# Attention layer of a four-layer network: Q, K and V in seven block products each, with t in the output's pixel order

## The chip, the cores and the metric

The kernel is one program on 1 core of one Trainium2 chip. The metric is device microseconds (us) of that core from launch to end; lower is better. Shown times are medians over several executions.

## The reference

Four layers follow one another, each of the form `x = x + layer(groupnorm(x))` on a float32 image batch of 8 x 16 x 256 x 256. Layer 0 is a convolution with capsule routing, layer 1 a convolution over spline bases, layer 2 an attention, layer 3 a circular 3x3 convolution. The change is in layer 2 alone:

```
hn, wn = (H // P, W // P)          # P = 16: 256 patches of 16 x 16 pixels
N = hn * wn;  ed = P * P
emb = _pos_embeddings(C * N, ed).reshape(C, N, ed)
patches = x.reshape(B, C, hn, P, wn, P).transpose(0, 1, 2, 4, 3, 5).reshape(B, C, N, ed)
t = (patches + emb[None]).transpose(0, 1, 3, 2)
Q = t @ Wq.T + bq
K = t @ Wk.T + bk
V = t @ Wv.T + bv
score = jnp.einsum('bcph,bcpg->bchg', K, Q) / np.float32(HID ** 0.5)
A = jax.nn.sigmoid(score)
out = jnp.einsum('bcph,bchg->bcpg', V, A)
```

For each of the 8 x 16 = 128 pairs of image and channel ("heads" below), t, Wq, Wk, Wv, score and A are 256 x 256 matrices. So a head has five products of 256 x 256 by 256 x 256, all in float32.

## The kernel before, in words

The four layers run one after the other. All matmuls are float32, and the profile shows each as two records on TensorE, each with its own weight load.

**Layer 2** is the method `layer2`. It loops over images and, within an image, over 16 channels, and calls `attend` once for each head. A 256-row operand lies in SBUF as two halves of 128 partitions. In one head:

- VectorE (DVE) makes t from the patches `pt` by one subtract-and-multiply (L1525), and GpSimd (POOL) adds the position table `emb` (L1529).
- Q and K come together: four matmuls of 512 columns into two PSUM tiles `pqk` (L1535); DVE adds the bias and writes `qk` (L1536).
- V comes transposed: four matmuls of 256 columns into `pv` (L1542); ScalarE (ACT) adds the bias in four pieces that also put V's columns in pixel order (L1546).
- Scores: four matmuls of 256 columns into `psc` (L1550), and one sigmoid on ACT (L1558).
- Output: four matmuls of 256 columns into `po` (L1562). DVE adds the residual and writes the row tile `y` (L1567), takes its statistics (L1574, L1575), POOL copies the two edge columns (L1576, L1577), and SyncE (SP) issues the store of `y` to the scratch array `x3` (L1578).

**Order.** In layer 2 only SP's queue is written out by hand (`manual_schedule(engines={SP})`); on the other engines the framework's scheduler orders the instructions. PE's order comes out as pqk x3, pv x4, psc x4, pqk x1 (of the next head), po x4, so that work of the next head stands between a head's scores and its output.

**Buffers.** The PSUM pool has two buffers of each of `pqk`, `pv`, `psc` and `po`, all eight banks. In SBUF the pools `l2_t` and `l2_mid` have two buffers each, except `y`, which has three: head i's `y` can be written when the store of head i-3 has landed.

**SP's queue.** Besides the stores it issues the residual rows (`rows`, four channels at a time, at channels 2, 6, 10 and 14), and at channel 3 the whole patches of the next image (`patches`, two DMAs, L1427), which land in the one of the two `pt` tiles that is not in use. In the last image it fetches the first inputs of layer 3 instead (`first3`, channels 4 to 12). Its order around channel 3 is: the store of channel 2, the two patch loads, the store of channel 3.

**Statistics.** The statistics of the layer's input come in two parts: those of the last image are finished during image 1 (`stats2_steps`, all steps at once), and layer 3's during the last image (`stats3`).

Of the kernel before, what the change touches and what calls it, by code (L numbers as in the profile page):

```python
# [10 lines left out]
F32 = mybir.dt.float32  # L11
AF = mybir.ActivationFunctionType
ALU = mybir.AluOpType
AX = mybir.AxisListType
PSUM = bass.MemoryType.PSUM
DRAM = bass.MemoryType.DRAM

B, C, H, W = 8, 16, 256, 256
P = 128
WP = W + 2  # L20
# [101 lines left out]
def _embedding():  # L122

    n = 256
    pos = np.arange(C * n, dtype=np.float32)[:, None]
    step = np.float32(-(np.log(10000.0) / n))
    div = np.exp(np.arange(0, n, 2, dtype=np.float32) * step).astype(np.float32)
    ang = (pos * div).astype(np.float32)
    emb = np.zeros((C * n, n), np.float32)
    emb[:, 0::2] = np.sin(ang)  # L130
    emb[:, 1::2] = np.cos(ang)
    emb = emb.reshape(C, 2, P, 2, 8, 16)
    return np.ascontiguousarray(emb.transpose(2, 1, 0, 4, 3, 5)).reshape(P, 2, C, n)


def _layout(w0, bw, sw, sc, bias, wq, bq, wk, bk, wv, bv, w3):
# [156 lines left out]
class _Net:  # L293
# [1138 lines left out]
    def layer2(self, images=range(B), channels=range(C)):  # L1432

        nc, tc = self.nc, self.tc
        images = list(images)
        with ExitStack() as st:
            self.tpool = st.enter_context(tc.tile_pool(name="l2_t", bufs=2))
            one = st.enter_context(tc.tile_pool(name="l2_one", bufs=1))
            load = st.enter_context(tc.tile_pool(name="l2_load", bufs=2))
            mid = st.enter_context(tc.tile_pool(name="l2_mid", bufs=2))  # L1440
            wqk, wv, bqk, bv = (self.w2[name] for name in ("qk", "v", "bqk", "b2v"))
            self.pt.append(one.tile([P, 2, C, 8, 32], F32, name="pt1"))
            emb = one.tile([P, 2, C, 256], F32, name="emb")
            first = load.tile([P, 4, 16, 2, 16], F32, name="res2")
            nc.sync.dma_start(out=emb[:, :, 1:4], in_=self.d["emb"][:, :, 1:4])
            nc.sync.dma_start(
                out=first.rearrange("p c n k j -> p c (n k j)"),
                in_=self.x2[images[0]][0:4].rearrange("c r h n k j -> (r h) c (n k j)"),
            )
            nc.sync.dma_start(out=emb[:, :, 4:C], in_=self.d["emb"][:, :, 4:C])  # L1450
            psum = st.enter_context(tc.tile_pool(name="l2_ps", bufs=2, space=PSUM))
            stats = self.st3

            def bank():
                t = []

                def get():
                    if not t:
                        t.append(psum.tile([P, 512], F32, name="pb2", tag="po"))
                    return t[0]  # L1460

                return get

            def patches(b):

                pt = self.pt[b % 2]
                for half in range(2):
                    self.patch(b, half, 0, C)
                return pt

            def rows(b, c):

                res = load.tile([P, 4, 16, 2, 16], F32, name="res2")
                nc.sync.dma_start(
                    out=res.rearrange("p c n k j -> p c (n k j)"),
                    in_=self.x2[b][c : c + 4].rearrange("c r h n k j -> (r h) c (n k j)"),
                )
                return res

            pts, ress = {images[0]: self.pt[images[0] % 2]}, {(images[0], 0): first}  # L1480
            with tc.manual_schedule(engines={mybir.EngineType.SP}):
                for n, b in enumerate(images):
                    after = images[n + 1] if n + 1 < len(images) else None
                    for c in channels:
                        if c in (2, 6, 10):
                            ress[b, c // 4 + 1] = rows(b, c + 2)
                        if c == 3 and after is not None:
                            pts[after] = patches(after)
                        if c == 14 and after is not None:
                            ress[after, 0] = rows(after, 0)  # L1490
                        if c == 2 and n == 1:

                            last, steps = self.stats2_steps(self.small, "g2b", bank)
                            for _, _, run, _ in steps:
                                run()
                        if c == 0 and after is None:
                            self.bc3 = self.stats3(bank, "g3a")
                        if 4 <= c < 13 and after is None:
                            self.first3(images[:2], c - 4)
                        bc = self.bc2 if after is not None else last  # L1500
                        e = self.emb0 if c == 0 else emb[:, :, c]
                        self.attend(mid, psum, b, c, pts[b], ress[b, c // 4], e, wqk, wv, bqk, bv, bc, stats)

    def first3(self, images, part):

# [5 lines left out]
    def weights3(self, ws, stat, b):  # L1511
        self.nc.vector.scalar_tensor_tensor(
            ws, self.w3, stat[0][:, 1, b : b + 1], self.k["ident3"], ALU.mult, ALU.add
        )

    def stats3(self, bank, name):
        out, steps = self.stats3_steps(self.small, name, bank)
        for _, _, run, _ in steps:
            run()
        return out  # L1520

    def attend(self, mid, psum, b, c, pt, res, emb, wqk, wv, bqk, bv, bc, stats):
        nc = self.nc
        t = self.tpool.tile([P, 2, 8, 32], F32, name="t")
        nc.vector.tensor_scalar(  # L1525
            t, pt[:, :, c], bc[:, 0, b, c : c + 1], bc[:, 1, b, c : c + 1], ALU.subtract, ALU.mult
        )
        t = t.rearrange("p h r f -> p h (r f)")
        nc.gpsimd.tensor_tensor(t, t, emb, ALU.add)  # L1529

        qk = mid.tile([P, 2, 512], F32, name="qk")
        for k in range(2):
            ps = psum.tile([P, 512], F32, name="pqk")
            for n in range(2):
                nc.tensor.matmul(ps, t[:, n, k * P : (k + 1) * P], wqk[:, n, :], start=n == 0, stop=n == 1)  # L1535
            nc.vector.tensor_tensor(qk[:, k, :], ps, bqk, ALU.add)  # L1536

        pv = psum.tile([P, 2, 256], F32, name="pv")
        vt = mid.tile([P, 2, 2, 8, 2, 8], F32, name="vt")
        for k in range(2):  # L1540
            for n in range(2):
                nc.tensor.matmul(pv[:, k], wv[:, n, k * P : (k + 1) * P], t[:, n, :], start=n == 0, stop=n == 1)  # L1542
        for k in range(2):
            src = pv[:, k].rearrange("p (r i o s) -> p o s i r", r=8, i=2, o=2)
            for o in range(2):
                nc.scalar.activation(vt[:, k, o], src[:, o], AF.Identity, bias=bv[:, k : k + 1])  # L1546
        ps = psum.tile([P, 2, 256], F32, name="psc")
        for k in range(2):
            for n in range(2):
                nc.tensor.matmul(  # L1550
                    ps[:, k],
                    qk[:, n, 256 + k * P : 256 + (k + 1) * P],
                    qk[:, n, 0:256],
                    start=n == 0,
                    stop=n == 1,
                )
        a = mid.tile([P, 2, 256], F32, name="a")
        nc.scalar.activation(a, ps, AF.Sigmoid, scale=1.0 / 16.0)  # L1558
        po = psum.tile([P, 2, 256], F32, name="po")
        for o in range(2):  # L1560
            for k in range(2):
                nc.tensor.matmul(  # L1562
                    po[:, o], vt[:, k, o].rearrange("p s i r -> p (s i r)"), a[:, k, :], start=k == 0, stop=k == 1
                )
        y = mid.tile([P, 2, WP], F32, name="y2", bufs=3)
        rows = y[:, :, 1 : 1 + W]
        nc.vector.tensor_tensor(  # L1567
            rows.rearrange("p o (n j) -> p o n j", j=16),
            po.rearrange("p o (n j) -> p o n j", j=16),
            res[:, c % 4].rearrange("p n k j -> p k n j"),  # L1570
            ALU.add,
        )
        i = b * C + c
        nc.vector.bn_stats(stats[0][:, i, :], rows)  # L1574
        nc.vector.bn_aggr(stats[1][:, :, i], stats[0][:, i])  # L1575
        nc.gpsimd.tensor_copy(y[:, :, 0:1], y[:, :, W : W + 1])  # L1576
        nc.gpsimd.tensor_copy(y[:, :, WP - 1 : WP], y[:, :, 1:2])  # L1577
        nc.sync.dma_start(out=self.x3[b][:, c].rearrange("r h k w -> r h (k w)"), in_=y.rearrange("p k w -> p (k w)"))  # L1578

    def fetch3(self, engines, b, xs, part=range(9)):

# [175 lines left out]
def _arrays(  # L1759
# [31 lines left out]
        )  # L1791
    )
    return {"x": np.ascontiguousarray(x), "consts": _consts(), "emb": _embedding(), **made}


# [14 lines left out]
```

## Time and profile before

| | us |
|---|---|
| three runs: lowest, median, highest | 6235.46, 6244.17, 6245.69 |
| the profiled execution | 6237.4 |
| its span in the profile | 6235.3 |
| layer 0, about | 121 to 3243 of the span |
| layer 1, about | 3311 to 4865 |
| layer 2, first to last `y` | 4879.5 to 5997.4 |
| layer 3, about | 6003 to 6235 |
| PE busy in 4880 to 5997 (1117 us) | 1114.59 |
| DVE, ACT, POOL busy there | 422.86, 229.18, 197.61 |

The mean granted TensorE clock is 0.987 of full speed, and 1.00 in layer 2. The span is the time from the first to the last instruction that the profiler saw; 2.1 us of the execution lie around it. A profile line gives line, engine, operation, out<-in, shapes, count, busy time and the mean of one in ns, then the idle time before it and who ended it. A busy PE is a modelled figure, since matmuls overlap; the spacing of their starts says more.

### The profile page before, as it was taken

The numbers are of one execution on the slowest core, as the hardware profiler recorded it, in microseconds if no ns is written. First come the engines' busy times: TensorE is split into PE (matmuls) and PEld (weight loads), VectorE is DVE, ScalarE is ACT, GpSimd is POOL, SyncE is SP. The second block draws the span as 40 slices with busy tenths as digits, with TensorE's granted clock in tenths as the row PEclk, the third lists the DMA queues.
The fourth block names the chain that finished last, engine by engine and source line by source line (L and its number), as shares of the span: only waits on it lengthen the run. The fifth ranks groups of instructions, "written<-read, shape, count | busy, mean of one in ns | idle before, by whom it ended". The sixth has DMA issues, their size and how long they took to land.

```text
span 6235.3 us, 111335 instructions
## 1 busy us (share of the span) xinstructions
PE 5930.8 (95%) x44488; PEld 2760.5 (44%) x44488; DVE 4895.1 (79%) x5771; ACT 3073.6 (49%) x4858; POOL 3593.7 (58%) x3040
## 2 busy tenths in 40 slices
PE   2999999999999999999968999999999999999998
PEld 0344444444444444444423444444444666666652
DVE  5799999999999999999968999999999433333321
ACT  0444544444454445444427888888888222111221
POOL 0588888888888888888873333434443111111123
PEclk9999999999999999999978999999999999999999
DMA  7455555555555555555516555555557443444358
GB/s 286 120 137 126 144 140 134 132 144 137 130 139 142 136 126 146 138 133 133 129 40 194 177 175 176 179 175 173 175 177 191 116 90 85 89 94 103 87 183 255
DMA packets 408790, 902.08 MB, mean 145 GB/s; under 512 B 62034, under 2 KB 195762, under 8 KB 364882
## 3 DMA queue, kind: packets, MB, share of 16 engines
q1 hardware_dynamic: 364434, 831.69, 48.8%
q10 hardware_dynamic: 33984, 34.08, 1.7%
q0 software_dynamic: 9856, 29.20, 1.7%
q8 instruction: 351, 5.75, 0.4%
q14 instruction: 165, 1.35, 0.1%
HBM read 684.09 MB, written 210.77 MB: 144 GB/s over the span
## 4 chain that ended last, share of the span: by engine, by line
PE 59%; DVE 26%; issue 7%; DMA 4%; POOL 3%; ACT 1%; SPq 0%; DVEq 0%; POOLq 0%; ACTq 0%
PE rb L831 8%; PE cv L587 7%; PE pqk L1535 7%; DVE bases L1089 7%; PE pl L733 6%; DVE e L1079 4%; PE cv L591 4%; PE po L1562 4%; PE cv L550 4%; PE pv L1542 4%; PE psc L1550 4%; PE p L1627 3%; DVE pr L723 2%; DVE a L1079 2%; DVE e L1058 2%
## 5 line engine op out<-in xcount | busy, mean ns | idle before, releaser
L1112 PE MATMUL ps<-bases,tw 128*32 128x512 f32 (+1 forms) x13824 | 1360.1, 546 | 16.5 <-POOL bases L1081 6.5
L851 POOL TENSOR_TENSOR dd<-dd 128x1024 f32<-128x1024 f32 x512 | 1210.9, 2365 | 70.9 <-DVE dd L842 65.6
L1081 POOL TENSOR_TENSOR bases<-e,a 128x1024 f32<-128x1024 f32 (+1 forms) x264 | 621.1, 2375 | 925.6 <-DVE e L1079 925.6
L723 DVE TENSOR_TENSOR pr<-v,fb 128x2048 f32<-128x2048 f32 (+1 forms) x512 | 1020.8, 2014 | 17.1 <-PE pl L733 12.6
L1112 PEld LDWEIGHTS ps<-bases,tw 128*32 128x32 f32 x13824 | 597.7, 109 | 800.3 <-issue 483.3
L842 DVE SCALAR_TENSOR_TENSOR dd<-rb,v 128x1024 f32<-128x1024 f32 x768 | 906.5, 1214 | 8.9 <-POOL dd L851 3.3
L851 POOL TENSOR_TENSOR s<-s,dd 128x512 f32<-128x512 f32 x512 | 647.0, 1274 | 15.1
L831 PE MATMUL rb<-rs,ct_fold 32*128 32x512 f32 x3072 | 592.9, 634 | 25.6 <-DVE pr L723 20.2
L1546 ACT ACTIVATE vt<-pv,w_b2v 128x128 f32<-128x128 f32 x512 | 146.1, 368 | 839.6 <-PE pv L1542 839.6
L733 PE MATMUL pl<-pr,ct_fold 128*32 128x512 f32 x3584 | 506.9, 603 | 4.3 <-DVE pr L723 4.3
L587 PE MATMUL cv<-kt,w 128*128 128x512 f32 x1024 | 497.2, 608 | 11.0 <-DMA kt<-d 9.8
L851 POOL TENSOR_TENSOR s<-v,dd 128x512 f32<-128x512 f32 x256 | 328.6, 1283 | 292.5 <-DVE dd L842 292.5
L1535 PE MATMUL pqk<-w_qk,t 128*128 128x512 f32 x1024 | 482.7, 594 | 4.6 <-POOL t L1529 4.6
L550 PE MATMUL cv<-kt,w 128*128 128x512 f32 x1024 | 477.4, 609 | 2.5 <-DMA kt<-d 2.5
L1567 DVE TENSOR_TENSOR y<-po,res 128x512 f32<-128x512 f32 x128 | 88.5, 691 | 490.1 <-PE po L1562 476.0
L1529 POOL TENSOR_TENSOR t<-t,emb 128x512 f32<-128x512 f32 x128 | 162.1, 1267 | 515.8 <-DVE t L1525 501.4
L1089 DVE SCALAR_TENSOR_TENSOR bases<-xr,xm,bases 128x1024 f32<-128x1024 f32 (+1 forms) x264 | 446.5, 1729 | 0.3 <-POOL bases L1081 0.3
L596 ACT COPY v<-cv 128x1024 f32<-128x1024 f32 x256 | 251.8, 1007 | 303.1 <-PE cv L591 303.1
L1066 ACT ACTIVATE sq<-a 128x1024 f32<-128x1024 f32 (+1 forms) x264 | 263.8, 999 | 230.2 <-DVE a L1058 229.5
L831 PEld LDWEIGHTS rb<-rs,ct_fold 32*128 32x128 f32 x3072 | 226.1, 185 | 325.5 <-issue 129.3
L697 PEld LDWEIGHTS fb<-f,ct_fold 64*128 64x128 f32 x3072 | 208.7, 188 | 310.5 <-issue 177.0
L842 DVE SCALAR_TENSOR_TENSOR dd<-r,v 128x512 f32<-128x512 f32 x256 | 176.9, 691 | 190.8 <-PE r L831 176.3
(281 smaller groups left out, 10164.7 us busy)
## 6 DMA issues: line engine op xcount, KB each, us to landing
xr<-x1p SPq DMA_DIRECT2D x120, 1024.0 KB
kt<-d SPq DMA_DIRECT2D x256, 387.0 KB
kt<-d SPq DMA_DIRECT2D x128, 516.0 KB
d<-dn ACTq DMA_DIRECT2D x64, 516.0 KB
kr<-d SPq DMA_DIRECT2D x128, 258.0 KB
kt<-d SPq DMA_DIRECT2D x128, 258.0 KB
x<-y SPq DMA_DIRECT2D x128, 258.0 KB
xs<-in_x_dram SPq DMA_DIRECT2D x16, 2048.0 KB
```

Source lines behind the costliest of these rows:

```text
L550: nc.tensor.matmul(ps[g]()[:, n], w[:, 0], t[:, a : a + 2, 0:W], start=False, stop=True)
L587: nc.tensor.matmul(ps()[:, n], w2[:, 0, j, :], t[:, a : a + 2, 0:W], start=True, stop=False)
L723: nc.vector.tensor_tensor(pr()[:, :n].rearrange("p n (r w) -> p n r w", w=W), v[h]()[:, 4 * g : 4 * g + n].rearrange("p n (r w) -> p n r w ...
L733: nc.tensor.matmul(pl()[at : at + 32], sel[:, g, h, :], pr()[:, t, :], start=h == 0 and g == 0, stop=h == 1 and (g == 1 or t == 3),)
L831: nc.tensor.matmul(r()[:, n], spread[at, g, h, :], rs()[at], start=True, stop=True)
L842: nc.vector.scalar_tensor_tensor(dd()[:, :n], r()[:, :n], 1.0 / B, v[h]()[:, a : a + n], ALU.subtract, ALU.mult)
L851: op("POOL", us, lambda: nc.gpsimd.tensor_tensor(out[0](), a[0](), b[0](), ALU.add), a[1] + b[1], out[1])
L1079: nc.vector.tensor_tensor(q, q, part[4 + k], ALU.mult)
L1081: nc.gpsimd.tensor_tensor(ring[n % 3][:, 0, p : p + m, 1 : 1 + W], rows(e), rows(a), ALU.subtract)
L1089: nc.vector.scalar_tensor_tensor(r, rows(part[1]), xm[:, b : b + 1], v, ALU.is_gt, ALU.mult)
L1112: nc.tensor.matmul(out if k is None else out[:, k], lhs, rhs, start=start, stop=stop, skip_group_check=True)
L1535: nc.tensor.matmul(ps, t[:, n, k * P : (k + 1) * P], wqk[:, n, :], start=n == 0, stop=n == 1)
```

## The change

Q and K are treated as the product of t (256 x 256) with the two weight matrices, each cut into 2 x 2 blocks, and so is V. Instead of the eight block products of the schoolbook method, seven are made, of sums of blocks; the blocks of the result are sums of these. The four sums of t's blocks, `ds`, are made once for each head on POOL and serve Q, K and V. The sums of the weights' blocks, `wt` and `wu`, are made once for the layer on DVE. Q's and K's weights are the two column blocks (of 256 columns) of one 256 x 512 matrix; a block product has 256 columns there, and 128 for V. Some block products land in a PSUM tile that is read by DVE first and is accumulated into after that (`rest`, `values_rest`).

The columns of t and of `emb` now lie in the pixel order of the output, so DVE makes t in two instructions that read `pt` in strides, and V needs no reordering.

`attend` is gone. The order of all engines is written out by hand: in the step of head i, t and `ds` of head i+1, the products of head i, the output of head i-1, the scores of head i. `psum` has one buffer of each tile (`po`: two), `qk`, `a`, `u2` and `g2` have one, and `y` has two instead of three. The statistics' steps are spread, one PE step for each head.

```diff
-    return np.ascontiguousarray(emb.transpose(2, 1, 0, 4, 3, 5)).reshape(P, 2, C, n)
+    return np.ascontiguousarray(emb.transpose(2, 1, 0, 5, 3, 4)).reshape(P, 2, C, n)
...
-            psum = st.enter_context(tc.tile_pool(name="l2_ps", bufs=2, space=PSUM))
+            psum = st.enter_context(tc.tile_pool(name="l2_ps", bufs=1, space=PSUM))
...
+            wt = one.tile([P, 4, 256], F32, name="wt")
+            nc.vector.tensor_tensor(wt[:, 0], k0, q0, ALU.subtract)
+            nc.vector.tensor_tensor(wt[:, 1], k1, wt[:, 0], ALU.subtract)
...
+            def prepare(b, c):
...
+                t = ts[b, c] = self.tpool.tile([P, 2, 256], F32, name="t")
+                for h in range(2):
+                    nc.vector.tensor_scalar(
+                        t[:, h].rearrange("p (n i r) -> p n i r", i=2, r=8),
+                        pts[b][:, h, c].rearrange("p r (i n) -> p n i r", i=2),
...
+                nc.gpsimd.tensor_tensor(t, t, self.emb0 if c == 0 else emb[:, :, c], ALU.add)
+                d = sums[b, c] = self.tpool.tile([P, 4, P], F32, name="ds")
+                a11, a12, a21, a22 = t[:, 0, :P], t[:, 1, :P], t[:, 0, P:], t[:, 1, P:]
+                nc.gpsimd.tensor_tensor(d[:, 0], a21, a22, ALU.add)
+                nc.gpsimd.tensor_tensor(d[:, 1], d[:, 0], a11, ALU.subtract)
+                nc.gpsimd.tensor_tensor(d[:, 2], a11, a21, ALU.subtract)
+                nc.gpsimd.tensor_tensor(d[:, 3], a12, d[:, 1], ALU.subtract)
...
+            def product(b, c):
...
+                mm(ps[0], t[:, 0, :P], q0, True, True)
+                mm(ps[1], d[:, 1], wt[:, 1], True, True)
+                mm(ps[2], d[:, 2], wt[:, 2], True, True)
+                mm(ps[3], d[:, 0], wt[:, 0], True, True)
...
+                nc.vector.tensor_tensor(u, ps[0].unsqueeze(1).to_broadcast([P, 2, 256]), both, ALU.add)
+                nc.vector.tensor_tensor(u, ps[1].unsqueeze(1).to_broadcast([P, 2, 256]), u, ALU.add)
+                nc.vector.tensor_tensor(last, ps[2], u[:, 1], ALU.add)
+                nc.vector.tensor_tensor(last, ps[3], last, ALU.add)
...
+            def rest(b, c):
...
+                mm(ps[0], t[:, 1, :P], q1, False, True)
+                mm(ps[2], t[:, 1, P:], wt[:, 3], False, True)
+                mm(ps[3], d[:, 3], k1, False, True)
+                nc.vector.tensor_tensor(qk[:, 0, :256], ps[0], bqk[:, :256], ALU.add)
+                nc.vector.tensor_tensor(qk[:, 1, :256], ps[2], u[:, 0], ALU.add)
+                nc.vector.tensor_tensor(qk[:, 0, 256:], ps[3], u[:, 1], ALU.add)
+
+            def values(b, c):
...
+                mm(pv[:, 0], v00, t[:, 0, :P], True, True)
+                mm(pv[:, 1], wu[:, 1], d[:, 1], False, True)
+                mm(pv[:, 2], wu[:, 2], d[:, 2], False, True)
+                mm(pv[:, 3], wu[:, 0], d[:, 0], False, True)
...
+                nc.scalar.activation(g, pv[:, 0], AF.Identity)
+                nc.vector.tensor_tensor(g, pv[:, 1], g, ALU.add)
+                nc.vector.tensor_tensor(last, pv[:, 2], g, ALU.add)
+                nc.vector.scalar_tensor_tensor(last, pv[:, 3], bv[:, 1:2], last, ALU.add, ALU.add)
...
+            def values_rest(b, c):
...
+                mm(pv[:, 0], v10, t[:, 1, :P], False, True)
+                mm(pv[:, 2], wu[:, 3], t[:, 1, P:], False, True)
+                mm(pv[:, 3], v11, d[:, 3], False, True)
+                nc.scalar.activation(vt[:, 0, :P], pv[:, 0], AF.Identity, bias=bv[:, 0:1])
+                nc.vector.scalar_tensor_tensor(vt[:, 0, P:], pv[:, 2], bv[:, 0:1], g, ALU.add, ALU.add)
+                nc.vector.scalar_tensor_tensor(vt[:, 1, :P], pv[:, 3], bv[:, 1:2], g, ALU.add, ALU.add)
...
-        y = mid.tile([P, 2, WP], F32, name="y2", bufs=3)
+                y = mid.tile([P, 2, WP], F32, name="y2", bufs=2)
...
-            with tc.manual_schedule(engines={mybir.EngineType.SP}):
+            with tc.manual_schedule():
+                prepare(*todo[0])
+                for i, (b, c) in enumerate(todo):
...
+                    if i + 1 < len(todo):
+                        prepare(*todo[i + 1])
+                    product(b, c)
+                    values(b, c)
+                    rest(b, c)
+                    values_rest(b, c)
+                    if i:
+                        output(*todo[i - 1])
+                    step(late)
+                    step(after3)
+                    score(b, c)
+                output(*todo[-1])
```

`score` and `output` hold the same matmuls, sigmoid, residual add, statistics, edge copies and store as `attend` did.

## The prediction

> **What bounds the kernel now.** I read the table of windows first, by layer:
>
> ```profile
> 4880.00:5997.00 1117.00, 1114.59 (x4123) 763.27 (x4121) 422.86 (x791) 229.18 (x645) 197.61 (x379) 1.00 0.41 94
> ```
>
> In layer 2 (columns: window, us, then PE, weight loads, DVE, ACT, POOL, clock, DMA share, GB/s) PE is busy all the time at full clock and DVE for 38% of it. Then the timeline of one head, PE and DVE rows:
>
> ```profile
> 5208.31 0.55 DVE L1525 TENSOR_SCALAR t<-pt,g2a_bc 128x512 f32<-128x512 f32 x1 [1.11 <-PE pv L1542]
> 5209.76 1.02 PE L1535 MATMUL pqk<-w_qk,t 128*128 128x512 f32 x2
> 5210.67 2.00 PE L1562 MATMUL po<-a,vt 128*128 128x256 f32 x8
> 5212.50 2.74 PE L1535 MATMUL pqk<-w_qk,t 128*128 128x512 f32 x6
> 5212.70 0.69 DVE L1567 TENSOR_TENSOR y<-po,res 128x512 f32<-128x512 f32 x1 [3.85 <-PE po L1562]
> 5213.43 0.69 DVE L1574 BATCH_NORM_STATS2 st<-y 128x6 f32<-128x512 f32 x1
> 5215.08 1.89 PE L1542 MATMUL pv<-t,w_v 128*128 128x256 f32 x8
> 5216.80 0.59 PE L1550 MATMUL psc<-qk 128*128 128x256 f32 x2
> 5217.08 0.55 DVE L1525 TENSOR_SCALAR t<-pt,g2a_bc 128x512 f32<-128x512 f32 x1 [1.11 <-PE pv L1542]
> ```
>
> The period is 5217.08 - 5208.31 = 8.77 us. PE starts follow without holes: six records of 512 columns from 5212.50 to 5215.08, 0.429 us each; eight of 256 from 5215.08 to 5216.80, 0.216 each. A head has 8 and 24: 3.43 + 5.18 = 8.61, and about 0.16 is lost where `po` waits for the sigmoid. DVE idles 3.85 us before `y`. So PE's stream is the bound, and DVE has slack.
>
> SP's queue around channel 3 of image 3, and DVE's `y` there:
>
> ```profile
> 5319.02 0.57 SPq L1578 DMA_DIRECT2D x<-y  x1
> 5320.14 15.78 SPq L1427 DMA_DIRECT2D pt<-x  x2
> 5336.03 15.28 SPq L1578 DMA_DIRECT2D x<-y  x3
> 5344.24 0.69 DVE L1567 TENSOR_TENSOR y<-po,res 128x512 f32<-128x512 f32 x1 [3.85 <-PE po L1562]
> 5353.59 0.69 DVE L1567 TENSOR_TENSOR y<-po,res 128x512 f32<-128x512 f32 x1 [4.42 <-DMA x<-y]
> ```
>
> The patches' two issues hold SP for 15.8 us, so channel 3's store, whose `y` was made at 5326.70, is issued at 5336.03; it lands at 5353.5 by its semaphore. Three heads later the `y` that takes its buffer starts at 5353.59, released by that DMA: with three buffers this just fits.
>
> **The change part by part.**
>
> *PE's work.* Q and K: 7 x 2 records of 256 columns instead of 8 of 512: 3.02 for 3.43 us. V: 7 x 2 records of 128 columns instead of 8 of 256. Nearest row, 96 columns with full 128x128 weights:
>
> ```profile
> L1210 PEld LDWEIGHTS ps<-bases,ct_ident x18: 190/192/192, 3305.0 to 3306.9; 128*128 128x128 f32 x18
> L1210 PE MATMUL ps<-bases,ct_ident x18: 246/275/276, 3305.1 to 3306.9; 128*128 128x96 f32 x18
> ```
>
> The starts stand 0.112 apart (L1202, 144 columns: 0.122), although a load takes 0.19: loads overlap each other and the matmuls. So V is 14 x 0.112 = 1.57 for 1.73. With scores and output (3.45) PE has 8.05 for 8.61 us: 0.56 less. The Trainium skill, "TensorE: Matmul & The Clock Gate", "What overlaps and what doesn't", says that a weight load overlaps a matmul in flight only if their row groups differ. All of V's loads take all rows; by that rule each record costs a load of some 0.11 more, 14 x 0.11 = 1.5 us a head, +197 us in all. The row shows full-array loads hidden, and I take the row.
>
> *DVE's work.* Rows: from PSUM 512 elements 0.69 (L1536, L1567), 256 0.425 (L1338), 128 0.277 (L1355), with a scalar 0.282 (L665). In the trace an independent DVE instruction starts 0.08 before the one ahead ends, one that needs its result 0.034 after, and 0.104 after where it also waits for another engine through a wait of its own (L787 behind L786). Per head: t twice, u 2 x 0.69, six of 256, five of 128, y, statistics 0.87: some 7.2 us for 3.5. Still below PE's, but now in a chain.
>
> *The chain.* PE's order is products, V's first four, the rest, V's rest, output of i-1, scores. V's rest must wait until DVE has read all of `pv`. From the head's start: products 4 x 0.432 and V 4 x 0.224 end at 2.62, `pv` complete at 2.78; ACT copies g (0.04 + 0.36) to 3.18; DVE adds pv1, pv2, pv3 (0.03 + 0.277 + 0.034 + 0.277 + 0.034 + 0.282) to 4.11; PE sees it and loads weights (0.10 + 0.11) at 4.33, where the stream would have been at 3.92: 0.4 us idle. Then 0.67 + 1.73 + 1.73: period 8.46.
> The second loop is DVE's: `y` of i-1 starts 0.27 after output's end, at 7.0; y and statistics 1.55, t twice, u 0.80 + 0.80, last 0.53 + 0.35, and only then pv1. With t at 0.41 (256 elements, L1094) pv1 may start at 3.2 of the next head, just when g is there. t's price is not in the trace, since it now reads with strides: 0.28 (L1058, 256 elements) to 0.546 (today's 512, no gain). At 0.28 the period stays 8.46, at 0.546 it is 8.74. By the nearest row 8.47. Strides and the waits behind PE's semaphores can only add: I take 8.55, with ends 8.42 and 8.80. 127 periods x (8.55 - 8.77) = -28 us (-44 to +4).
>
> *POOL.* Four `ds` of 0.456 (L675) more a head, 3.5 us of 8.55, done by 4.3 of the head before: hidden by a whole head. Without that cover products 2 to 4 would wait about 1 us a head.
>
> *`y` with two buffers.* Head i's `y` now waits for the store of i-2. SP's order around the patches is unchanged, one store between. In the trace the store of channel 3 lands later than the second next `y` starts, in images 0 to 6, by 2.1, 10.1, 1.6, 9.3, 1.5, 9.4, 1.7: 35.6 us (e.g. 5353.5 - 5344.24). A shorter period makes that `y` due three periods after the patches' start, 0.22 x 3 earlier: +4.6. All DVE work is behind that `y`, and PE's rest of the next head waits for DVE: no slack in the loop beyond 0.1, so +40 us. Less than zero it can't be; the upper end is 50.
> *The clock.* In the three long ones PE stands for about 8 us. After an idle time of 4.59:
>
> ```profile
> 4866.56 5.12 PE L1535 MATMUL pqk<-w_qk,t 128*128 128x512 f32 x8 [4.59 <-POOL t L1529]
> ```
>
> Eight records go from 4866.56 to 4871.52, 4.96 for 3.43: 1.5 us at half clock. 3 x 1.5 = +4.5 (0 to 6).
>
> *Ends.* Start: the first products wait for `ds` (two POOL steps of 0.53 behind t) and `wt`, and the first output is one step later: first `y` +2. End: the last output follows its own scores, 4.5 instead of a period: -4. Statistics: spread, but ACT's two table loads of 1.28 and the sigmoid's reload stand ahead of the next g and delay V's rest by some 2.9 us, twice; before, the two places cost 1.8 and 4.2: 0 (-2 to +2). `wt` and `wu`, 8 instructions, some 2 us once, lie beside POOL's first t and `ds`. Layer 3 is untouched.
>
> *Sum* against the profiled execution (6237.4): -28 + 40 + 4.5 + 2 - 4 = +14.5, so 6252. The median of the runs is 6.8 above it; there the same difference gives 6259.
>
> **The rivals.**
> *Main (0.52):* period 8.45 to 8.65, stalls as worked out: +4 to +25. What can be told from no change here is 0.2%, 12.5 us.
> *A, faster (0.22):* the late stores cost less than the heads gain. If channel 3's store lands before its buffer is wanted in most images, only the period counts: 127 x -0.22 - 2 = -30, 6214. It decides below 28 us of stalls. For it: in even images only 1.5 to 2.1 us are missing. Against: the patches' issue of 15.8 us and the order on SP are the same, and a shorter period makes it worse.
> *B, DVE becomes the bound (0.22):* t at no gain and a few waits more: period 8.80 to 9.0, +41 at the low end and +62 at the high: 6285 to 6306. For it: eleven dependent links, and a sum of 7.2 of 8.5. Against: each link has a row.
> *C, V's weight loads are exposed (0.04):* period about 10, some +200, 6440. L1210 speaks against it.
> That the change does not do what it says is no rival: the number of matmuls is in the code.
>
> **How the numbers follow.** The main case gives 6259. The range leaves out half of A's better part and C: 6222 to 6308. Of the main case two fifths lie within 12.5 us, of A a quarter. Slower 0.58, same 0.26, faster 0.16.
>
> **What would show it.** Right: starts of `y` 8.45 to 8.65 apart in most heads; idle PE of about 0.4 us before V's rest, released by DVE; in each of images 0 to 6 one `y` released by the DMA of a store, 2 us late in even images and 9 to 10 in odd ones, with PE idle and slow records behind the long ones; `pv` records 0.112 apart. Wrong: no `y` released by a DMA, or one that PE doesn't feel (A); DVE without idle time before `y` and `u` waiting for DVE alone (B); `pv` records over 0.2 apart (C).

## The result

| | us | against the kernel before |
|---|---|---|
| before, median of 4 runs | 6244.93 (6235.46 to 6246.46) | 1 |
| after, median of 4 runs | 6277.74 (6275.0 to 6278.53) | 1.0059 (95%: 1.0044 to 1.0074) |
| predicted | 6259 (6222 to 6308) | |

The changed kernel is slower by 0.59%: 32.8 us between the medians. The profiled execution took 6278.5 us, 41.1 more than that of before, where the prediction's sum gave 14.5. Of the difference 3.3 us lie before layer 2 and -2.8 after it; the rest is layer 2 and its start: from the first to the last `y` it takes 1153.2 us instead of 1117.9.

The table of windows of the changed kernel, for layer 2 (the columns are those of the row shown of before):

```profile
4888.00:6041.00 1153.00, 1084.15 (x5627) 897.79 (x5625) 883.06 (x2175) 165.53 (x389) 416.29 (x879) 0.99 0.40 91
```

PE was busy in all but 2.4 us of 1117; now it stands for 69 of 1153, though it has less to do. DVE went from 38% to 77%. The clock is no longer 1.00 throughout. So the layer has lost its plain bound, and the next views must say what PE waits for. The waits of the changed kernel in layer 2 (in all, times, longest):

```profile
DVE y L1609 <- issue: 91.5, 117, 1.6
...
DVE y L1609 <- DMA x<-y: 34.1, 5, 11.2
...
PEld pq L1520 <- DVE u L1534: 31.6, 9, 9.5
...
PE pv L1520 <- DVE vt L1567: 29.0, 122, 0.2
```

Two different things are here. 122 times PE waits 0.24 us ahead of V's rest for DVE: in nearly every head. And five times `y` waits for the store that frees its buffer, up to 11.2 us, and PE waits for `u`, which stands behind that `y` on DVE, up to 9.3. The five are the `y` of channel 4 in images 1, 2, 3, 5 and 6. In images 0 and 4 the same `y` is late too, by 2.6 and 2.1 us, but this view names another releaser there.

The first, in the timeline of one head of the changed kernel:

```profile
5203.15 1.89 PE L1604 MATMUL po<-a,vt 128*128 128x256 f32 x8
...
5205.14 0.69 DVE L1609 TENSOR_TENSOR y<-po,res 128x512 f32<-128x512 f32 x1 [0.78 <-issue]
...
5206.60 0.59 PE L1520 MATMUL pq<-w_qk,t 128*128 128x256 f32 x2
5206.69 0.90 DVE L1503 TENSOR_SCALAR t<-pt,g2a_bc 128x256 f32<-128x256 f32 x2
...
5207.49 0.69 DVE L1534 TENSOR_TENSOR u<-pq,w_bqk 128x512 f32<-128x512 f32 x1
...
5210.18 0.67 PE L1520 MATMUL pq<-w_qk,ds 128*128 128x256 f32 x2
...
5210.59 0.35 DVE L1567 SCALAR_TENSOR_TENSOR vt<-pv,w_b2v,vt 128x128 f32<-128x128 f32 x1
...
5211.09 0.46 PE L1520 MATMUL pv<-t,w_v 128*128 128x128 f32 x2 [0.24 <-DVE vt L1567]
...
5211.83 1.89 PE L1604 MATMUL po<-a,vt 128*128 128x256 f32 x8
```

This is a closed loop through DVE and PE. `y` (5205.14) is followed on DVE, with gaps of at most 0.11 us, by its statistics, t, u, two additions of `qk` and those of `pv` as far as L1567 (5210.59, 5.45 later); V's rest on PE follows at 5211.09 (0.50); output stands behind V's rest (5211.83, 0.74); and an undelayed `y` starts 1.99 after output does, as 5205.14 - 5203.15 shows for the output ahead of it. 5.45 + 0.50 + 0.74 + 1.99 = 8.68, and the starts of `y` are 8.67 to 8.68 apart in most heads. The PE stream has a hole in it: the last two records of the rest start at 5210.18 and take 0.43, so V's rest could start at 5210.61 and starts 0.48 later.

The second, around channel 4 of image 3 in the changed kernel (SP's queue, DVE, PE):

```profile
5332.06 14.76 SPq L1427 DMA_DIRECT2D pt<-x  x1
...
5346.93 19.84 SPq L1620 DMA_DIRECT2D x<-y  x3
...
5365.10 0.69 DVE L1609 TENSOR_TENSOR y<-po,res 128x512 f32<-128x512 f32 x1 [11.24 <-DMA x<-y]
...
5368.18 1.22 PE L1520 MATMUL pq<-w_qk,t 128*128 128x256 f32 x2 [9.29 <-DVE u L1534]
...
5369.50 1.22 PE L1520 MATMUL pq<-wt,t 128*128 128x256 f32 x2
```

The issue of the second patch load lasts until 5346.82; that of the store of channel 2, behind it, begins at 5346.93, and the store has landed at 5364.98 by its semaphore; the `y` of channel 4, which takes that buffer, starts at 5365.10. DVE keeps its order, so t, u and the additions start after that, and PE stands for 9.29 us and then runs its records at half speed (1.22 for two records that take 0.60 in other heads; the granted clock is 0.50 from 5361.5 to 5371.7).

### The profile page after: what moved, and what is told of

The parts are those of the page before. It is cut to its first block, busy times and chain, and to the rows that moved or that the text cites. A ratio compares the mean times of both kernels' runs of the same rounds, so it can differ in the third digit from the quotient of the medians.

```text
span 6276.5 us, 117259 instructions
## 1 busy us (share of the span) xinstructions
PE 5906.9 (94%) x46024; PEld 2902.3 (46%) x46024; DVE 5368.3 (86%) x7187; ACT 3010.6 (48%) x4602; POOL 3821.4 (61%) x3552
## 4 chain that ended last, share of the span: by engine, by line
PE 46%; DVE 35%; issue 9%; DMA 5%; POOL 3%; ACT 2%; DVEq 0%; SPq 0%; POOLq 0%; ACTq 0%
PE rb L831 8%; PE cv L587 7%; DVE bases L1089 7%; PE pl L733 6%; DVE e L1079 4%; PE cv L591 4%; PE cv L550 4%; PE p L1717 3%; DVE pr L723 2%; PE po L1604 2%; DVE a L1079 2%; DVE a L1058 2%; DVE e L1058 2%; PE pv L1520 2%; PE fb L697 2%
## 5 line engine op out<-in xcount | busy, mean ns | idle before, releaser
L1112 PE MATMUL ps<-bases,tw 128*32 128x512 f32 (+1 forms) x13824 | 1360.4, 545 | 15.9 <-POOL bases L1081 6.5
L596 ACT COPY v<-cv 128x1024 f32<-128x1024 f32 x256 | 251.9, 1008 | 302.4 <-PE cv L591 302.4
L1618 POOL COPY y<-y 128x2 f32<-128x2 f32 x128 | 24.1, 189 | 521.0 <-DVE y L1609 521.0
L1048 ACT ACTIVATE d<-xr,bd,sd 128x1024 f32<-128x1024 f32 (+1 forms) x264 | 319.1, 1209 | 14.2 <-DMA xr<-x1p 14.2
L572 ACT COPY v<-cv 128x1024 f32<-128x1024 f32 x256 | 258.1, 1008 | 139.4 <-PE cv L550 139.3
L550 PEld LDWEIGHTS cv<-kt,w 128*128 128x128 f32 x1024 | 184.5, 190 | 290.9 <-issue 281.8
```

The source lines that it names most:

```text
L550: nc.tensor.matmul(ps[g]()[:, n], w[:, 0], t[:, a : a + 2, 0:W], start=False, stop=True)
L1112: nc.tensor.matmul(out if k is None else out[:, k], lhs, rhs, start=start, stop=stop, skip_group_check=True)
```

## The experiments

The main theory: the period is set by the loop above, which runs through DVE; the stalls come from the late stores, and cost what they do because all of DVE's work stands behind `y`. Its rivals: PE's own stream sets the period (as before); the buffers alone make the stall, whatever the order; the stores are late because of bytes, not because of SP's queue.

Layer 2 is read from the starts of `y` in each profile: the first to the last (free of what layers 0, 1 and 3 do), the median of the 127 distances, and the distances that exceed it. The ratios are against the runs of the kernel before on the same chip (medians 6238.2, 6238.8 and 6237.8 us in three groups); in them the changed kernel's 1.0059 would be 6275.

| kernel | time, us | ratio (95%) | first to last `y` | period |
|---|---|---|---|---|
| before | | 1 | 1117.9 | 8.77 |
| after | | 1.0059 (1.0044 to 1.0074) | 1153.2 | 8.68 |
| 1: three buffers of y | 6238.0 | 0.9997 (0.9989 to 1.0005) | 1113.3 | 8.63 |
| 2: before, two buffers | 6241.5 | 1.0006 (0.9998 to 1.0015) | 1122.7 | 8.77 |
| 3: t without strides | 6264.0 | 1.0038 (1.0025 to 1.0050) | 1136.6 | 8.50 |
| 4: one more product | 6281.9 | 1.0069 (1.0055 to 1.0082) | 1158.2 | 8.68 |
| 5: late y at channel 4 | 6253.8 | 1.0022 (1.0014 to 1.0030) | 1127.9 | 8.68 |
| 6: loads apart | 6237.3 | 0.9994 (0.9986 to 1.0003) | 1116.5 | 8.68 |
| 7: 1, and output ahead of V's rest | 6161.1 | 0.9872 (0.9856 to 0.9889) | 1042.5 | 8.04 |
| 8: 7, and t on ACT | 6161.7 | 0.9873 (0.9859 to 0.9888) | 1036.9 | 8.04 |
| 9: 6, and output ahead of V's rest | 6159.4 | 0.9871 (0.9855 to 0.9888) | 1038.5 | 8.05 |
| 10: 7, and loads apart | 6154.1 | 0.9864 (0.9849 to 0.9879) | 1035.1 | 8.04 |
| 11: 9, no root in the statistics | 6153.9 | 0.9863 (0.9848 to 0.9878) | 1031.7 | 8.05 |

### 1. Three buffers of y

```diff
-                u = mid.tile([P, 2, 256], F32, name="u2", bufs=1)
-                qk = qks[b, c] = mid.tile([P, 2, 512], F32, name="qk", bufs=1)
+                qk = qks[b, c] = mid.tile([P, 4, 256], F32, name="qk", bufs=1)
+                u = qk[:, 1:3]
...
-                y = mid.tile([P, 2, WP], F32, name="y2", bufs=2)
+                y = mid.tile([P, 2, WP], F32, name="y2", bufs=3)
```

> The changed kernel with three buffers for y again; to find the room, u lies in the two middle quarters of qk, and nothing else is moved. Theory 1 (with two buffers, the y of channel 5 waits for channel 3's late store, and that wait is on the path): the stalls of 35 to 43 us of images 0 to 6 go, so 6235 to 6245 us, -33 to -43 against the changed kernel and within 0.2% of the kernel before; no y is released by a DMA for more than 2 us in all, and y's period stays 8.67. Theory 2 (the stalls are only where waiting becomes visible, and the heads that follow would have stood anyway for POOL or for the loads of patches): at most -10 us, about 6268, and idle time of the same length appears before t, ds or the products.

From 1.0059 to 0.9997, and 39.8 us less in layer 2, as theory 1 has it. Of these, 127 x 0.045 = 6 are a shorter period (`y` starts 0.72 us after DVE's last work instead of 0.78) and 34 are stalls. The waits of this kernel in layer 2 have instead of 34.1 us in five:

```profile
DVE y L1609 <- DMA x<-y: 5.8, 2, 3.2
```

With three buffers images 3 and 5 still lose 1.9 and 2.4 us at channel 5, more than was expected; that a head of 8.63 leaves a little less room than one of 8.77 would explain it, and was not tested. The stalls did not come back elsewhere.

### 2. Two buffers in the kernel before

```diff
-        y = mid.tile([P, 2, WP], F32, name="y2", bufs=3)
+        y = mid.tile([P, 2, WP], F32, name="y2", bufs=2)
```

> The kernel before with two buffers of y instead of three: that one part of the change alone. Theory 1: the y of channel 5 waits for channel 3's store by the 35.6 us read from the trace of before. The kernel before has 3.85 us of idle DVE ahead of y and its output stands a step earlier against PE's stream, so a wait of about 2 us may be hidden in part: +30 to +45 us, 6275 to 6290. Theory 2 (TensorE's stream goes on while y waits, because po has two buffers): under +10 us, 6255 at most.

Theory 1 fails here: no change that can be told from zero, and 4.8 us in layer 2. The wait itself is there. The `y` of channel 5 comes 3.1 us late in images 0, 2, 4 and 6 and 9.8 to 10.6 late in images 1, 3 and 5; but the next one or two distances are short by almost all of it (18.70, 1.87, 7.09 in image 3, which is 27.66 where three heads take 26.31). DVE's rows there, and PE's scores:

```profile
5347.00 0.55 DVE L1525 TENSOR_SCALAR t<-pt,g2a_bc 128x512 f32<-128x512 f32 x1 [1.11 <-PE pv L1542]
5352.25 0.69 DVE L1536 TENSOR_TENSOR qk<-pqk,w_bqk 128x512 f32<-128x512 f32 x1 [4.71 <-PE pqk L1535]
5353.97 0.69 DVE L1536 TENSOR_TENSOR qk<-pqk,w_bqk 128x512 f32<-128x512 f32 x1 [1.02 <-PE pqk L1535]
5361.38 0.69 DVE L1567 TENSOR_TENSOR y<-po,res 128x512 f32<-128x512 f32 x1 [6.72 <-DMA x<-y]
...
5363.25 0.66 DVE L1567 TENSOR_TENSOR y<-po,res 128x512 f32<-128x512 f32 x1
...
5365.28 2.22 PE L1550 MATMUL psc<-qk 128*128 128x256 f32 x8 [0.86 <-DVE qk L1536]
```

In other heads the order on DVE is `y`, statistics, the two `qk`. Here the framework's scheduler has put both `qk` of the next head ahead of the waiting `y`. With those, and with t made a head ahead and two PSUM buffers of `pqk`, PE has over a head of work while DVE waits, and loses 0.86 us and some slower records (2.07 us for eight that take 1.73 in other heads, at a granted clock of 1.00). So two buffers and a store some 10 us late cost 1.4 us there and over 10 in the order written out by hand. The buffer is a condition of the stall, not its whole cause.

### 3. t without strides

```diff
-                        t[:, h].rearrange("p (n i r) -> p n i r", i=2, r=8),
-                        pts[b][:, h, c].rearrange("p r (i n) -> p n i r", i=2),
+                        t[:, h],
+                        pts[b][:, h, c].rearrange("p r f -> p (r f)"),
```

> The changed kernel with t written and read in one run of addresses instead of in strides (its columns then do not stand in the order that the position table has, so that the sums are of other pixels; the work is the same in kind and number). Theory 1 (DVE's loop sets the period of 8.67, and t's strides cost 0.21 us an instruction): t falls from 0.49 to about 0.28 us, DVE's loop by 0.42, and the period to 8.46, where the chain through V's rest takes over: -24 to -28 us, about 6252. Theory 2 (PE's stream with its 0.24 us wait sets the period, and DVE's work lies beside it): t is as short, but the period stays 8.65 or more, -3 us or less. Theory 3 (t's price is PSUM's or an instruction's own, not the strides'): t stays at 0.45 or more and nothing moves.

The rows of t in this kernel, in layer 2 (busy, mean ns), against 486 and 488 ns in the changed kernel:

```profile
L1503 DVE TENSOR_SCALAR t<-pt,g2a_bc 128x256 f32<-128x256 f32 x216 | 76.1, 395 | 0.0
L1503 DVE TENSOR_SCALAR t<-pt,g2b_bc 128x256 f32<-128x256 f32 x32 | 11.4, 400 | 0.0
```

The period follows t one to one: 2 x 0.091 less on DVE, and 8.50 instead of 8.675. That is theory 1's direction at half its size: the strides cost 0.09 us an instruction, not 0.21. (The Trainium skill's page "SBUF — State Buffer", in the remark on 16-byte lines in its section "Door 1: The DMA port swizzle", says that each access that crosses to a new line pays; it gives no size. The run agrees in direction: 0.09 us for 256 elements that were read 128 bytes apart.) Layer 2 falls by 16.6 us and not by 127 x 0.175 = 22: at channel 4 of images 0 to 6 the distances exceed the period by 38.5 us in all instead of 35.2, and the last image loses 2.2 more.

### 4. One more product

```diff
                 mm(ps[3], d[:, 3], k1, False, True)
+                mm(ps[1], t[:, 1, :P], q1, True, True)
```

> The changed kernel with one more block product of 256 columns (two records, 0.43 us of PE a head; its result is not used) put between Q's and K's rest and V's rest, where PE waits for DVE. Theory 1 (DVE's loop sets the period): of the 0.43 us only what exceeds the wait of 0.24 us and its weight load reaches V's rest, and DVE has about 0.8 us of idle time before y to take it: period 8.67 to 8.74, 0 to +8 us. Theory 2 (PE's stream sets the period, as in the kernel before): +0.43 us a head, +55 us, about 6333. Theory 3 (mixed, the loop runs through PE and DVE both): in between, about +25.

The period stays 8.68 with 0.43 us more on PE in each head; layer 2 takes 5.0 us more, not 55, as theory 1 has it. PE's work no longer sets the time: an eighth product for Q and K fits into the hole of 0.48 us.

### 5. The y of channel 4 later

```diff
-                        output(*todo[i - 1])
+                        o = output(*todo[i - 1], hold=todo[i - 1][1] in (4, 5))
+                        if todo[i - 1][1] == 4:
+                            held[4] = o
+                        elif todo[i - 1][1] == 5:
+                            finish(*todo[i - 2], *held[4])
+                            finish(*todo[i - 1], *o)
```

> The changed kernel, with two buffers of y, but in every image DVE's, POOL's and SP's work on the y of channel 4 (add, statistics, edge columns, store) stands one head later, just ahead of that of channel 5; PE's order is as it was. The kernel before with two buffers waited 18.7 - 8.77 = 10 us for the same store and gave it back in the next two heads, because its order there had put both qk additions of the next head ahead of that y. Theory 1 (the wait costs because all DVE work of the loop stands behind it; the buffers alone are not it): y's period of 19.13, 18.36 and 10.7 to 11.3 at channel 4 is replaced by one of at most 11 in odd images and 9.5 in even ones: -25 to -33 us against the changed kernel, about 6248. Theory 2 (one buffer of pq and pv instead of two makes PE stop in any case when y is late): at most -8 us, about 6270.

25.2 us less in layer 2: theory 1, at the low end of what it expected. In images 0, 2, 4 and 6 the two `y` now take 16.30 + 1.55 = 17.85 where two heads take 17.36, so the stall is gone to half a microsecond. In images 3 and 5 the store still lands after the later place, and 5 to 6 us are left of 11. With experiment 2 this shows what makes a late store dear: where `y` stands in DVE's order.

### 6. The two loads apart

```diff
-                    if c == 3 and after is not None:
-                        pts[after] = patches(after)
+                    if c in (3, 5) and after is not None:
+                        pts[after] = patches(after, c // 4)
```

> The changed kernel, with two buffers of y, and the two loads of the next image's patches issued at channels 3 and 5 instead of both at channel 3. Theory 1 (the stores are late because the two issues hold SP's queue for 15.8 us): each now holds it 7.9 us, less than a head, so a store is late by 0 to 2 us in odd images and not at all in even ones: -30 to -40 us, about 6242. Theory 2 (the stores are late because the patches' bytes stand ahead of them in the DMA rings, wherever they are issued): the lateness is cut in two and comes twice, so about -5 to -10 us, 6270.

The stalls are gone altogether, with two buffers of `y`: no `y` waits for a DMA, and layer 2 takes 36.6 us less. So the late stores come from the two issues standing one behind the other. But the way in which SP is held is not the expected one. SP's queue in image 3 of this kernel:

```profile
5318.58 0.72 SPq L1427 DMA_DIRECT2D pt<-x  x1
5326.07 9.25 SPq L1619 DMA_DIRECT2D x<-y  x2
5335.90 0.72 SPq L1427 DMA_DIRECT2D pt<-x  x1
5343.42 8.58 SPq L1619 DMA_DIRECT2D x<-y  x1
```

A load's own issue takes 0.72 us. It is the next issue that is held: the store at 5326.07 for 8.36 us, until 5334.4, which is 15.9 after the load's issue, when the load's data land (5333.8 to 5335.8 by its semaphore). In the changed kernel the second load is held 14.76 us behind the first, and the store is then held 14.46 behind the second, until 5361.4. Two loads together hold back a store for 30 us; each alone does so for 16, and the part of that in which SP would have waited for `y` anyway costs nothing. Since the hold lasts about as long as the load ahead, this run does not part SP's queue from the bytes ahead of it as the reason for the hold; it shows that the two loads back to back are what makes the store late.

### 7 and 8. Output ahead of V's rest, and t on ACT

```diff
-                    values_rest(b, c)
                     if i:
                         output(*todo[i - 1])
+                    values_rest(b, c)
```

> The kernel with three buffers of y (6238.0, y period 8.63), and the output of head i-1 put ahead of V's rest of head i in the order of PE and DVE; it is the one thing that differs from that kernel. Between the rest and V's rest PE then has the output's 1.73 us to do while DVE makes pv ready. Theory 1 (the loop through DVE's u, g and pv additions and V's rest sets the 8.63): PE's stream without its 0.5 us hole ahead of V's rest is 8.12, DVE's work of some 7.5 fits: period 8.12 to 8.25, -48 to -65 us against 6238.0, about 6180. Theory 2 (DVE's work alone fills the period, 8.63 whatever the order): -5 us or less. Theory 3 (y now stands ahead of V's rest on DVE and vt comes later, so that the next head's additions are late): some heads longer, 8.5 or more.

> As the kernel with three buffers of y and the output ahead of V's rest, and t (0.49 us twice a head on DVE) made on ACT with scale and bias, which idles for most of a head. Theory 1 (PE's stream is the bound once V's rest no longer waits): period 8.12 or a little less, and equal to the one with t on DVE to within 0.1 us: 6170 to 6185. Theory 2 (DVE's sum of work is the bound): the period falls by up to 0.9 us below that with t on DVE, until PE's 8.12 stops it.

The period goes from 8.63 to 8.04, a little lower than expected. Output, which needs nothing of this head, now fills the time in which DVE makes `pv` ready, and `y` no longer stands behind V's rest. A head of kernel 9, which has the same order with two buffers:

```profile
5200.94 0.59 PE L1519 MATMUL pq<-w_qk,t 128*128 128x256 f32 x2
...
5202.67 0.38 PE L1519 MATMUL pv<-t,w_v 128*128 128x128 f32 x2
...
5203.56 0.60 PE L1519 MATMUL pq<-w_qk,t 128*128 128x256 f32 x2
...
5204.88 1.89 PE L1603 MATMUL po<-a,vt 128*128 128x256 f32 x8
...
5206.60 0.38 PE L1519 MATMUL pv<-t,w_v 128*128 128x128 f32 x2
...
5207.27 1.89 PE L1587 MATMUL psc<-qk 128*128 128x256 f32 x8
...
5209.00 0.59 PE L1519 MATMUL pq<-w_qk,t 128*128 128x256 f32 x2
```

The distances are 1.73, 0.89, 1.32, 1.72, 0.67 and 1.73: the sum is PE's work alone, 8.06, without a hole. With t on ACT the median is the same 8.04, so DVE is not the bound any more; of the 5.6 us less in layer 2, 5.0 are in image 1 and the last image, where the statistics are.

### 9 and 10. The two moves together

> The changed kernel with two buffers of y as it has them, the output of head i-1 ahead of V's rest of head i, and the two patch loads issued at channels 3 and 5: nothing but those two moves. Theory 1 (the two causes are apart: the loop of the additions sets the period, the held SP queue the stalls): period 8.04, no stall at channel 4, and the 3.9 and 4.9 us that images 3 and 5 still lost with three buffers go too: 6161 - 9 = about 6152, -125 us against the changed kernel. Theory 2 (with heads of 8.04 us the load's 7.9 us on SP no longer leave room for two buffers): y waits for a DMA again by 1 to 8 us in each of seven images, 6160 to 6190.

> The kernel before this one with three buffers of y (u in qk's middle quarters). Theory 1: with the loads apart the number of buffers is worth nothing, so the two agree within 4 us. Theory 2: three buffers take away what two still wait for, 8 us or more below the one with two.

Kernel 9 is the changed kernel with its two buffers and two moves of a few lines. It is at 0.9871 of before, 1.9% below the changed kernel. The two causes are apart, as theory 1 has it: the stalls are gone by the loads, the hole by the order. One `y` still waits 1.0 us for a DMA, where others wait some 0.7 for output. The time is 7 us above theory 1's 6152, and layer 2's 1038.5 is 5 above the sum that this came from: the last image takes 1.6 of these, the period of 8.050 for 8.038 takes 1.5, and a few heads of 8.40 most of the rest. Kernel 10 takes 3.4 us less in layer 2, within what was expected; the intervals of the ratios overlap.

### 11. No root in the statistics

```diff
-            nc.scalar.activation(r, v, AF.Ln)
-            nc.scalar.activation(r, r, AF.Exp, scale=-0.5)
+            nc.vector.tensor_scalar(r, v, 0.0, 1.0, ALU.mult, ALU.add)
```

> As the one with the two moves and two buffers, with the reciprocal root of the variance in the statistics' steps left out: a constant, written by DVE in one instruction, takes the place of ACT's Ln and Exp. So there are no table loads in the statistics; layers 1 and 3 lose theirs as well, so layer 2 is read by itself. Theory 1 (image 1's 6.4 us above the period, and part of the last image's 6.4, come from ACT's table loads, which stand ahead of the sigmoid and of g): image 1 keeps at most 2.5 us and the last image loses 3 to 4: -7 to -8 us in layer 2. Theory 2 (they come from the statistics' own DVE and PE instructions between the heads): -2 us or less.

6.8 us less in layer 2, just short of theory 1: image 1's excess goes from 5.9 to 2.6, the last image's from 8.0 to 5.2. ACT in image 1 of kernel 9:

```profile
5033.62 1.28 ACT L1292 ACT_TABLE_LOAD   x1
5035.14 1.28 ACT L1293 ACT_TABLE_LOAD   x1
5036.66 1.28 ACT L1595 ACT_TABLE_LOAD   x1
5037.95 0.60 ACT L1595 ACTIVATE a<-psc 128x512 f32<-128x512 f32 x1
5038.45 0.27 ACT L1563 ACTIVATE g<-pv 128x128 f32<-128x128 f32 x1
```

The sigmoid starts 11.4 us after that of the head before (5026.52) and `g` 9.4 after its last (5029.07), where a head takes 8.05: three loads stand ahead of both. Of the 16.8 us by which image 1 and the last image exceed their heads in kernel 9 (its last distance, 5.14, set aside) the root accounts for 6.1, somewhat over a third. In kernel 8, with t off DVE, the two places lose 5.0 less than in kernel 7, so DVE's work has a share in the rest; that rest was not taken apart.

## Why the prediction was right, and where it was short

Direction and range hold, but the main case did not reach as far. It allowed +4 to +25 us and a period of up to 8.65; the medians are 32.8 us apart and the period is 8.68. By the medians the result lies between the main case and rival B's low end of +41, so the range held because it took in B's part, and B's cause, a period of 8.80, did not come. That is luck in part: period, statistics and start all missed to the same side, and the late stores to the other. By its own steps, against the profiled execution:

| step | predicted | measured | from |
|---|---|---|---|
| period of a head | -28 | -12 | 127 x (8.675 - 8.77) |
| late stores, with the half clock behind them | 40 + 4.5 | 36.6 | after less kernel 6, first to last `y` |
| statistics | 0 | +11 | image 1 +5.4 and last image +11.5 (kernel 6), less 1.8 and 4.2 before |
| start | +2 | +7 | layer 1's end to first `y`: 15.2 to 20.6; second `y` 1.8 later too |
| end | -4 | -4 | last distance 4.47 |
| small ones (heads of 9.02) | | +2 | kernel 6 |
| layers 0, 1 and 3, not touched | | +0.5 | +3.3 before layer 2, -2.8 after it |
| sum | +14.5 | +41 | |

*The late stores* were the right mechanism and nearly the right size: 2.0 to 2.6 us in images 0, 2, 4 and 6, 11 in 3 and 5, with PE idle and slow behind the long ones. Two details differ. It is the `y` of channel 4 that waits for channel 2's store, since output comes one head later than before. And in image 1 only 5 us are left of 10, presumably because the statistics have already delayed the heads before, so that the store had time. The reason given, "no slack in the loop", is the right one, and experiment 2 is its other half: where the order leaves slack, a wait as long is nearly free. The price in the row of before (how late the store is) was therefore not yet a price of two buffers.

*The period* is the term of the sum that was mis-sized, 8.68 for 8.55. The chain's 8.47 was built from the right links. From pv1 to V's rest on PE it had 1.12 us, and the trace has 1.14. t's step, from the end of the statistics to u, was about 0.65 in that sum (twice 0.41, with starts that overlap by 0.08) and is 0.80; from V's rest to `y` 2.67, and it is 2.73, of which kernel 1, with the third buffer and u inside qk, takes off 0.05. Together they are the 0.21. The allowance of 0.08 for strides and waits was too small by 0.13: strides alone cost 0.18 a head (experiment 3). Without strides t still takes 0.395 us and not 0.28; why was not tried. Rival B had the side of it right: DVE's additions are in the loop that sets the time, though its period of 8.80 was not reached. (The list of DVE's work has "six of 256" where the code has five; its sum of 7.2 is right with five.)

*PE's work* was right: 8.05 predicted, 8.04 to 8.05 measured once the hole is gone (kernels 7 to 10), with `pv` records 0.112 apart at full-array weights. So rival C, and the rule weighed there, is excluded by a run: with that rule the head would have been some 1.5 us longer by the prediction's estimate, and 2.7 with the 0.19 us that the trace shows for a load.

*The statistics* at 0 was wrong. The table loads were named, but set against what the two places cost before, as if they were the same cover. Before, PE's loop had DVE idle for 3.85 us ahead of `y`; the new loop has 0.78. Experiments 8 and 11 show that DVE's work and the table loads each cost time at these two places; how the 11 us divide in the changed kernel itself was not tested. *The start* was too low by 5: the first `y` now follows the products of a whole further head. This is read from the trace and was not tested.

*Rival A*, that the late stores cost less than the heads gain, would have needed stalls below 28 us; they were 36.6, and the gain was only 12.

## What to carry to other kernels

When a change takes work from the engine that bounds a loop, write down the new loop link by link and ask which work needs nothing of this step and could fill the wait: here the output of the head before, moved ahead of the part that waits, took the ratio from 0.9997 to 0.9872. How late a transfer lands is not what the lateness costs: the cost is what stands behind the waiting instruction in its engine's order, and it was 1.4 us or some 10 for stores about equally late, by that order and what it leaves to the engine behind. Before buying buffers, look at what is queued ahead of the late store; two long loads issued one behind the other made it late, and moving one of them by two heads was worth as much as the third buffer.

## What the runs showed of the hardware that was not expected

- A long load does not hold SP by its own issue (0.72 us) but by the next one: a second load stood for 14.8 us and the store behind it for 14.5, each until about the time at which the load ahead landed (the first of its data by its semaphore at 5346.3 and 5361.9, the ends of the two issues at 5346.8 and 5361.4). What sets the length of the hold was not tested. The prediction had read the 15.8 us of the two issues as the whole hold, and the store's own long row as flight time.
- Full-array weight loads of 0.19 us with 128-column records stay hidden at 0.112 us a record, also within whole heads of 14 such records and 30 of 256 columns (kernel 9: 8.05 from `y` to `y`, 8.06 as the sum of the distances).
- DVE took 0.487 us for 256 elements read in strides from SBUF with two scalar operands, 0.395 in one run of addresses (experiment 3).
